# A graph transformer layer on one core: loads of node rows at most eight chunks ahead, released by ScalarE

## The chip, the cores and the metric

The kernel runs on one core of one Trainium2 chip. The metric is the device time of one execution in microseconds (us); the number given for a kernel is the median of several executions. The core has five engines that follow their own instruction queues and meet at semaphores: TensorE (PE, with its weight loads listed as PEld), VectorE (DVE), ScalarE (ACT), GpSimd (POOL) and SyncE (SP), which only issues DMAs here.

## The reference

Three layers of a graph transformer convolution over 6250 nodes with 64 features. There are 206250 directed edges, sorted by their destination; each has its own 64 attributes.

```
q = x @ Wq + bq;  k = x @ Wk + bk;  v = x @ Wv + bv;  e = edge_attr @ We
alpha = sum(q[dst] * (k[src] + e)) / sqrt(64)
p = exp(alpha - segment_max(alpha, dst)[dst])
w = p / segment_sum(p, dst)[dst]
out = segment_sum((v[src] + e) * w, dst) + x @ Ws + bs
```

Between the layers come a ReLU and a layer norm; behind the last one a log softmax, the residual and a final layer norm. What costs time is `x[src]`: for every edge and in every layer, a row of 64 numbers from a place given by the graph. The kernel works with the rows of x and the edge attributes side by side and multiplies by the weights afterwards.

## The kernel before, in words

**Tiling.** The edges are cut into 403 chunks of 512, each four tiles of 128. Four chunks are a batch (101 batches, the last of three chunks). The work runs in 102 units, a unit being a batch except at the end, where the last batch makes two; `NU` is 102, `LB` is 4, `T` is 4.

**A batch's data.** `feat` is a buffer for one batch: for each edge the row of x and the 64 attributes. There are five such buffers (`FB` = 5). `fetch` (L532) writes the attributes with one DMA of 512 KB on SyncE's queue. `gather` (L549) writes the rows of x for one chunk: for each tile of 128 edges one indirect DMA on GpSimd (L553), with the tile's 128 node numbers read from a list in SBUF, `src_a` for the first edges and `src_b` for all. These DMAs are called loads here. In layers 1 and 2 `x` is the earlier layer's output (the tile is named `x`), in layer 0 the input (`in_x`). Three tiles of a batch have no load: `pick` (L841) makes their rows from x in SBUF, with TensorE multiplying by one-hot matrices (L858, L849) and VectorE masking and adding up (L868, L871); `aim` (L818) makes the one-hot matrix `hot` (L825, L830). So a batch takes 13 loads, 15 early in layer 0, and 16 where nothing is picked, as in a layer's batch 0.

**Which load may start when.** A load must not overtake the use of the buffer that it writes. In addition the kernel holds the loads of a chunk back until a turn of TensorE has come: `release` (L569) copies the chunk's indices to a small tile `gate` (L576, VectorE, 128x4 integers; 24 such buffers), and the loads read their indices from there. So a load of GpSimd, whose queue would otherwise run ahead, waits for that copy, and the copy stands in VectorE's queue at the place where it was issued.

**A round.** The main loop (L1253) has one round `u` for each unit but the last two. The round adds up the messages of unit u-3 (`sums(u - 2)` does all units below u-2; L1150), which sets that buffer free: `room` (L1196) then issues the `fetch` of batch u+2 into it and puts its chunks on the list `pending`. It transposes the weights of unit u-2 (L1136, L1138) and makes the scores of unit u-1 (L1115 once a unit, L1117 for each chunk; L1124, L1126, L1128 are the running softmax). Then there are four turns: `turn(j)` (L1096) transposes chunk j of unit u's rows by TensorE (L1100 in layer 0, L1105 later) and copies the result to `featT` on ScalarE (L1101, L1108). Behind `turn(j)` stands `release(j+1)`, which lets chunk j of batch u+2 be loaded, eight chunks ahead of the turn. Between the turns lie parts of `pick`, `aim` and of the tasks in `step` and `close_up`. `ask` (L1063) reads a unit's queries (L1075) and `across` (L1088) moves the transposed attributes between layers, both on SyncE.

**Starts.** At the program's start, five batches are fetched and all their loads issued with no gate (L615 to L618): 79 loads. At a layer's end (L1294 to L1345) the same is done for the next layer, five batches and 68 loads, once all of the layer's output has been written. Round 0 follows, and the first batch that is gated is batch 5, in round 3.

**Order.** Each engine runs its instructions in the order in which the program issues them; nothing reorders them across engines. So the place of a call in the loop is the place of its instructions in each queue.

Of the kernel before, what the change touches and what calls it, by code (L numbers as in the profile page):

```python
# [10 lines left out]
I32 = mybir.dt.int32  # L11
# [7 lines left out]
P = 128  # L19
D = 64  # L20
L = 3
T = 4
# [9 lines left out]
LB = 4  # L32
FB = 5
# [381 lines left out]
def main_path(  # L415
# [53 lines left out]
    nc = tc.nc  # L469
# [14 lines left out]
    batches = [(c, min(LB, NC - c)) for c in range(0, NC, LB)]  # L484
    units = list(batches)
    if units[-1][1] > 1:
        c, m = units.pop()
# [15 lines left out]
    gates = ctx.enter_context(tc.tile_pool(name="gates", bufs=6 * LB))  # L503
    nodes = ctx.enter_context(tc.tile_pool(name="nodes", bufs=2))

    def ps(tag):
        return psum.tile([P, 512], F32, tag=tag, name=f"ps_{tag}", bufs={"a": 3, "x": 2}.get(tag, 1))
# [5 lines left out]
    def picked(layer, k):  # L513

        if batches[k][1] < LB or k < LEAD[layer]:
            return 0
        return 1 if layer == 0 and k <= len(groups) else PICKS
# [5 lines left out]
    HEAD = FB * LB * T  # L523
    src_a = const.tile([P, HEAD], I32, name="src_a")
    nc.sync.dma_start(src_a, src[:, :HEAD])
    src_b = const.tile([P, NC * T], I32, name="src_b")
    loaded = {}

    def fetch(layer, k):

        c0, m = batches[k]
        feat = feats.tile([P, LB * T * 2 * D], F32, name="feat")  # L532
        if layer:
            feat = feat.rearrange("p (h c t d) -> p c t h d", h=2, c=LB, d=D)
        else:
            feat = feat.rearrange("p (c t h d) -> p c t h d", h=2, c=LB, d=D)
        nc.sync.dma_start(
            feat[:, :m, :, 1].rearrange("p c t d -> p (c t) d"),
            ea[c0 : c0 + m].rearrange("c (t p) d -> p (c t) d", p=P),
        )  # L540
        loaded[layer, k] = feat

    def spots(n):

        return [(c, T - 1) for c in range(LB - n, LB)]

    def gather(layer, k, c, index, i):

        feat = loaded[layer, k]  # L549
        for t in range(T):  # L550
            if (c, t) in spots(picked(layer, k)):
                continue
            nc.gpsimd.indirect_dma_start(  # L553
                out=feat[:, c, t, 0],
                out_offset=None,
                in_=xts[layer][:, :],
                in_offset=bass.IndirectOffsetOnAxis(ap=index[:, i + t : i + t + 1], axis=0),
            )

    def gather_all(layer, k):  # L560

        c0, m = batches[k]
        index = src_a if (c0 + m) * T <= HEAD else src_b
        for c in range(m):
            gather(layer, k, c, index, (c0 + c) * T)

    pending = []

    def release(upto):  # L569

        for entry in list(pending):
            layer, k, c = entry
            c0, m = batches[k]
            while c < min(m, upto):
                gate = gates.tile([P, T], I32, name="gate")
                nc.vector.tensor_copy(gate, src_b[:, (c0 + c) * T : (c0 + c + 1) * T])  # L576
                gather(layer, k, c, gate, 0)
                c += 1
            entry[2] = c
            if c == m:  # L580
                pending.remove(entry)

    ident = const.tile([P, P], F32, name="ident")
    make_identity(nc, ident)
# [25 lines left out]
    def rows_of(g, n):  # L610
        y = nodes.tile([P, GS, D], F32, name="xr")[:, :n]
        nc.sync.dma_start(y, x[g * P : (g + n) * P, :].rearrange("(j p) d -> p j d", p=P))
        return y

    entered = {g: rows_of(g, n) for g, n in groups[:2]}  # L615
    for k in range(FB):
        fetch(0, k)
        gather_all(0, k)  # L618


    spans = dram.tile([NK * P, 2], F32, name="spans")
# [197 lines left out]
    def aim(layer, k):  # L819

        if k >= len(batches) or not picked(layer, k):
            return
        n = picked(layer, k)
        pk = ps("p")[:, : n * P]
        nc.tensor.matmul(  # L825
            pk, one[:, k : k + 1].to_broadcast([P, P]), keyT[:, (MOST - n) * P :], start=True, stop=True
        )
        for s in range(n):
            hot = picks.tile([P, NH, P], F32R, name="hot")
            nc.vector.tensor_tensor(  # L830
                hot,
                pk[:, s * P : (s + 1) * P].unsqueeze(1).to_broadcast([P, NH, P]),
                rank.unsqueeze(2).to_broadcast([P, NH, P]),
                ALU.is_equal,
            )
            hots[layer, k, s] = hot
# [85 lines left out]
    def begin(g, n):  # L922
        y = entered.get(g)
        if y is None:
            y = rows_of(g, n)
            yield
        yield from project(0, g, n, y)
# [241 lines left out]
    next(first)  # L1169
    rest = locate(0)  # L1170
    next(rest), next(rest)
    next(first, None)
    next(rest), next(rest)
    for _ in first:
        pass
    for _ in rest:
        pass
    nc.vector.tensor_copy(base, ends[:, :, 0])
    active.append(begin(*groups[1]))
    active.append(keys())  # L1180
    active.append(divide())
# [14 lines left out]
    def room(layer, k):  # L1196

        if k < len(batches):
            fetch(layer, k)
            pending.append([layer, k, 0])  # L1200
        elif layer + 1 < L and k - len(batches) < FB:
            fetch(layer + 1, k - len(batches))

# [37 lines left out]
    def close_up(n=1):  # L1241
        step(n)
        for _ in range(n):
            advance(ending)

    def some(picking):

        for _ in range(2):
            next(picking, None)

    ask(0, 0)
    chunks[0, 0].across()
    for layer in range(L):  # L1253
        line = Line(layer)
        assert not picked(layer, 0)
        aim(layer, 1)
        for u in range(NU - 2):
            close = u >= CLOSE
            this = chunks[layer, u]
            picking = pick(layer, u + 1)  # L1260
            line.sums(u - 2)
            line.weights(u - 1)
            line.scores(u)
            if waiting:
                active.append(waiting.pop(0))
            this.turn(0)
            release(1)
            close_up(2) if close else close_up()
            ask(layer, u + 1)
            chunks[layer, u + 1].across()  # L1270
            some(picking)
            aim(layer, u + 2)
            this.turn(1)
            release(2)
            line.store()
            close_up(2) if close else step()
            some(picking)
            if close:
                line.sums(u - 1)
                line.weights(u)  # L1280
            this.turn(2)
            release(3)
            line.store()
            close_up(2) if close else step()
            some(picking)
            if close:
                line.sums(u)
            line.store()
            assert next(picking, None) is None
            this.turn(3)  # L1290
            release(LB)
            close_up(2) if close else step()

        more = layer + 1 < L  # L1294
        assert not pending
        ask(layer, NU - 1)
        rest, last = chunks[layer, NU - 2], chunks[layer, NU - 1]
        line.scores(NU - 2)
        last.across()
        if more:  # L1300
            reload(layer + 1, 0)
            reload(layer + 1, 1)
            ask(layer + 1, 0)
        rest.turn(0)
        line.weights(NU - 2)
        close_up()
        for j in range(1, rest.m):
            rest.turn(j)
        if more:
            split(*held[0])  # L1310
        line.sums(NU - 2)
        line.store()
        close_up()
        line.scores(NU - 1)
        if more:
            chunks[layer + 1, 0].across()
            split(*held[1])
        line.weights(NU - 1)
        last.turn(0)
        close_up()  # L1320
        line.scores(NU)
        line.sums(NU - 1)
        line.store()
        line.weights(NU)
        line.sums(NU)
        line.store()
        while active or len(ending) > 1:
            close_up()
        if more:
            for i in range(2, len(pieces) - 1):  # L1330
                reload(layer + 1, i)
        while ending and (not more or (layer, groups[-1][0]) not in written):
            close_up()
        if more:
            assert all((layer, g) in written for g, n in groups)
            for k in range(FB):
                if (layer + 1, k) not in loaded:
                    fetch(layer + 1, k)
                gather_all(layer + 1, k)
            reload(layer + 1, len(pieces) - 1)  # L1340
            close_up()
            for i in range(2, len(pieces)):
                split(*held[i])
            while ending:
                close_up()  # L1345
# [45 lines left out]
```

## Time and profile before

| | |
|---|---|
| three executions, us | 7144.72, 7116.72, 7071.52 |
| median, us | 7116.72 |
| profiled execution, us | 7065.72 |
| its span, us | 7063.9 |
| its mean granted TensorE clock | 0.84 |
| loads by L553 without a gate | 79 in layer 0, 136 in layers 1 and 2 |
| loads by L553 with a gate | 1265 in layer 0, 2494 in layers 1 and 2 |
| gate copies by L576 | 1149 |
| one load on GpSimd, one gate copy on VectorE | 0.944 us, 0.161 us (medians) |

The profiled execution is one of its own and 0.7% below the median. In a line of the profile, the part in brackets is the time that the engine stood idle before the instruction, and what ended that. "issue" means that nothing in the profile explains the idle time, "remote" that what ended it is not an instruction that the profile shows. Of the lines that belong to the loads and to what stands beside them, these are the costliest:

```profile
L858 PE MATMUL ps_x<-parts,hot 128*128 128x512 f32 x10344 | 3109.7, 450 | 800.8 <-DVE rows_of_b L868 458.5
L553 POOL DMA_INDIRECT feat<-x,gate x2494 | 2360.8, 947 | 1944.0 <-issue 945.2
L553 POOL DMA_INDIRECT feat<-in_x,gate x1265 | 1200.2, 949 | 1038.6 <-issue 511.8
L868 DVE TENSOR_TENSOR rows_of_b<-ps_x,which 128x512 f32<-128x512 f32 x862 | 590.7, 685 | 1314.7 <-remote 863.4
L1108 ACT COPY featT<-ps_a 64x256 f32<-64x256 f32 x1612 | 589.3, 366 | 1659.2 <-remote 782.7
```

A line gives the place in the code, the engine, the operation with its tiles and shapes and how often it occurs; then its busy time in us and the mean ns of one; then the idle time of the engine just before it and what ended most of that.

### The profile page before, as it was taken

The numbers are of one execution on the slowest core, as the hardware profiler recorded it, in microseconds if no ns is written. First come the engines' busy times: TensorE is split into PE (matmuls) and PEld (weight loads), VectorE is DVE, ScalarE is ACT, GpSimd is POOL, SyncE is SP. The second block draws the span as 40 slices with busy tenths as digits, with TensorE's granted clock in tenths as the row PEclk, the third lists the DMA queues.
The fourth block names the chain that finished last, engine by engine and source line by source line (L and its number), as shares of the span: only waits on it lengthen the run. The fifth ranks groups of instructions, "written<-read, shape, count | busy, mean of one in ns | idle before, by whom it ended". The sixth has DMA issues, their size and how long they took to land.

```text
span 7063.9 us, 83912 instructions
## 1 busy us (share of the span) xinstructions
PE 5168.6 (73%) x24583; PEld 3500.1 (50%) x24583; DVE 3348.6 (47%) x6501; ACT 1369.1 (19%) x3267; POOL 3765.2 (53%) x3982
## 2 busy tenths in 40 slices
PE   3777788877787557777777777764777777877786
PEld 2355555555555345454555455443455555555553
DVE  3344544554454335444454445443455554555554
ACT  1111111111111112122121222221122222222222
POOL 4555555555555345555555555534555555555553
PEclk9688888888888779888888888877888888888887
DMA  5333333333333323333333333332333333333332
GB/s 123 92 80 79 80 79 80 78 74 79 78 80 74 75 58 83 76 79 79 77 84 77 75 74 80 77 79 50 81 73 80 79 82 75 83 77 84 83 83 59
DMA packets 1132753, 554.00 MB, mean 78 GB/s; under 512 B 946566, under 2 KB 1043964, under 8 KB 1113091
## 3 DMA queue, kind: packets, MB, share of 16 engines
q1 hardware_dynamic: 988834, 409.90, 25.3%
q0 software_dynamic: 127168, 130.47, 8.5%
q10 hardware_dynamic: 16288, 8.17, 0.5%
q8 instruction: 204, 3.34, 0.2%
q14 instruction: 259, 2.11, 0.1%
HBM read 451.48 MB, written 96.59 MB: 78 GB/s over the span
## 4 chain that ended last, share of the span: by engine, by line


## 5 line engine op out<-in xcount | busy, mean ns | idle before, releaser
L858 PE MATMUL ps_x<-parts,hot 128*128 128x512 f32 x10344 | 3109.7, 450 | 800.8 <-DVE rows_of_b L868 458.5
L553 POOL DMA_INDIRECT feat<-x,gate x2494 | 2360.8, 947 | 1944.0 <-issue 945.2
L858 PEld LDWEIGHTS ps_x<-parts,hot 128*128 128x128 f32 x10344 | 2179.0, 219 | 1421.6 <-DVE rows_of_b L868 514.3
L553 POOL DMA_INDIRECT feat<-in_x,gate x1265 | 1200.2, 949 | 1038.6 <-issue 511.8
L868 DVE TENSOR_TENSOR rows_of_b<-ps_x,which 128x512 f32<-128x512 f32 x862 | 590.7, 685 | 1314.7 <-remote 863.4
L871 DVE TENSOR_REDUCE feat<-rows_of_b 128x64 f32<-128x512 f32 x862 | 905.4, 1050 | 29.7
L1108 ACT COPY featT<-ps_a 64x256 f32<-64x256 f32 x1612 | 589.3, 366 | 1659.2 <-remote 782.7
L830 DVE TENSOR_TENSOR hot<-ps_p,rank 128x896 fp32r<-128x896 f32 x862 | 883.3, 1077 | 8.9 <-PE ps_p L825 5.6
L1150 PE MATMUL ps_g<-feat,probT 128*64 128x256 f32 x4848 | 653.0, 402 | 54.3 <-issue 33.5
L1138 DVE COPY probT<-ps_p 128x512 f32<-128x512 f32 (+2 forms) x306 | 208.5, 681 | 977.4 <-remote 606.7
L1117 PE MATMUL ps_s<-featT,q 128*32 128x512 f32 x2418 | 438.0, 641 | 269.2 <-ACT featT L1108 195.5
L1124 DVE TENSOR_REDUCE most<-ps_s 128x1 f32<-128x512 f32 (+2 forms) x306 | 210.5, 688 | 871.9 <-remote 526.8
L1150 PEld LDWEIGHTS ps_g<-feat,probT 128*64 128x64 f32 x4848 | 343.0, 142 | 288.9 <-issue 141.6
L1128 ACT ACTIVATE prob<-ps_s,part 128x512 f32<-128x512 f32 (+2 forms) x306 | 210.4, 688 | 1412.1 <-DVE part L1126 740.8
L1101 ACT COPY featT<-ps_a 128x512 f32<-128x512 f32 x403 | 228.7, 585 | 964.0 <-remote 370.3
L1105 PE MATMUL ps_a<-ident,feat 128*128 128x128 f32 x1612 | 351.6, 300 | 51.5 <-issue 24.1
L1100 PE MATMUL ps_a<-ident,feat 128*128 128x128 f32 x1612 | 287.8, 302 | 54.7 <-issue 53.1
L1105 PEld LDWEIGHTS ps_a<-ident,feat 128*128 128x128 f32 x1612 | 192.8, 150 | 267.5 <-issue 186.9
L1158 ACT COPY part<-ps_g 128x256 f32<-128x256 f32 (+2 forms) x306 | 113.8, 372 | 1047.4 <-remote 578.0
L1100 PEld LDWEIGHTS ps_a<-ident,feat 128*128 128x128 f32 x1612 | 200.8, 155 | 167.9 <-issue 134.8
L1117 PEld LDWEIGHTS ps_s<-featT,q 128*32 128x32 f32 x2418 | 62.5, 110 | 409.6 <-ACT featT L1108 229.7
L825 PE MATMUL ps_p<-keyT,one 128*128 128x384 f32 (+1 forms) x294 | 127.9, 435 | 179.0 <-DVE probT L1138 122.3
(145 smaller groups left out, 2632.6 us busy)
## 6 DMA issues: line engine op xcount, KB each, us to landing
feat<-in_ea SPq DMA_DIRECT2D x300, 512.0 KB
featT<-eaT SPq DMA_DIRECT2D x200, 512.0 KB
eaT<-featT SPq DMA_DIRECT2D x100, 512.0 KB
feat<-x,gate POOLq DMA_INDIRECT x2494
feat<-in_x,gate POOLq DMA_INDIRECT x1265
part<-part SPq DMA_DIRECT2D x1209, 16.2 KB
q<-qq SPq DMA_DIRECT2D x1209, 16.0 KB
both<-part SPq DMA_DIRECT2D x66, 260.0 KB
```

The costliest lines, as they stand in the source:

```text
L553: nc.gpsimd.indirect_dma_start(out=feat[:, c, t, 0], out_offset=None, in_=xts[layer][:, :], in_offset=bass.IndirectOffsetOnAxis(ap=index[: ...
L830: nc.vector.tensor_tensor(hot, pk[:, s * P : (s + 1) * P].unsqueeze(1).to_broadcast([P, NH, P]), rank.unsqueeze(2).to_broadcast([P, NH, P] ...
L858: nc.tensor.matmul(px[:, : b1 - b0, :].rearrange("p b d -> p (b d)"), hot[:, h, :], parts[:, i, b0:b1, :].rearrange("p b d -> p (b d)"), s ...
L868: nc.vector.tensor_tensor(rows, px, which[:, MOST - n + s, k, :].unsqueeze(2).to_broadcast([P, KB, D]), ALU.mult)
L871: nc.vector.tensor_reduce(loaded[layer, k][:, LB - n + s, T - 1, 0], rows.rearrange("p b d -> p d b"), AX.X, ALU.add)
L1100: nc.tensor.transpose(pt[:, t * P : (t + 1) * P], self.feat(j)[:, t].rearrange("p h d -> p (h d)"), ident)
L1101: nc.scalar.copy(self.featT[:, j, :], pt)
L1105: nc.tensor.transpose(pt[:, t // 2 * P : (t // 2 + 1) * P], rows[:, t * D : (t + 2) * D], ident)
L1108: nc.scalar.copy(featT[:, :, h, :], pt[h * D : (h + 1) * D, : T // 2 * P].rearrange("d (i e) -> d i e", e=P))
L1117: nc.tensor.matmul(self.p_s[j * W : (j + 1) * W, :], self.q[:, j, :], self.featT[:, j, :], start=False, stop=True)
L1124: nc.vector.tensor_reduce(top[:n], self.p_s[:n], AX.X, ALU.max)
L1150: nc.tensor.matmul(p_g[j * W : (j + w) * W, :w, :].rearrange("n c (h d) -> n c h d", h=2), self.probT[:, t, j * W : (j + w) * W], batch[:, ...
```

## The change

Three things are changed together.

- **Starts.** A layer's start issues the loads of batch 0 alone, 16 in place of 79 or 68. The other four batches are put on `pending`. In the program's start the `fetch` of batches 2 to 4 moves behind `ask(0, 0)` and `across`, and the four chunks of batch 1 are released one by one between the parts of the setup, by copies on VectorE.
- **Distance.** In the rounds, `free(u, j)` stands where `release(j+1)` stood. It releases every pending chunk whose number is below `u * 4 + j + 1 + lead`. `lead` is 8 chunks in layer 0, and the lesser of 8 and 4 + u in the others. From round 5 on this is one chunk a turn, 8 chunks ahead, as before; in rounds 1 to 4 of layers 1 and 2 it is five chunks a round, and in rounds 0 to 2, which released nothing, the chunks that a start no longer loads.
- **Engine.** The gate copies in the rounds are made by ScalarE in place of VectorE, right behind the turn's own copies in its queue.

The number of loads stays 3974. 1193 gate copies are issued on ScalarE and 4 on VectorE, where there were 1149 on VectorE. `fetch` of later batches stays where it was, in round u that of batch u+2.

```diff
+    def indices(layer, k, c):
+
+        c0, _ = batches[k]
+        if not layer and (c0 + c + 1) * T <= HEAD:
+            return src_a, (c0 + c) * T
+        return src_b, (c0 + c) * T
+
     def gather_all(layer, k):
 
-        c0, m = batches[k]
-        index = src_a if (c0 + m) * T <= HEAD else src_b
-        for c in range(m):
-            gather(layer, k, c, index, (c0 + c) * T)
+        for c in range(batches[k][1]):
+            gather(layer, k, c, *indices(layer, k, c))
 
     pending = []
 
-    def release(upto):
-
-        for entry in list(pending):
-            layer, k, c = entry
-            c0, m = batches[k]
-            while c < min(m, upto):
-                gate = gates.tile([P, T], I32, name="gate")
-                nc.vector.tensor_copy(gate, src_b[:, (c0 + c) * T : (c0 + c + 1) * T])
-                gather(layer, k, c, gate, 0)
-                c += 1
-            entry[2] = c
-            if c == m:
-                pending.remove(entry)
+    def await_turn(layer, k):
+
+        pending.extend((layer, k, c) for c in range(batches[k][1]))
+
+    def release(layer, upto, copy=nc.vector.tensor_copy):
+
+        while pending and pending[0][0] == layer and pending[0][1] * LB + pending[0][2] < upto:
+            layer, k, c = pending.pop(0)
+            index, i = indices(layer, k, c)
+            gate = gates.tile([P, T], I32, name="gate")
+            copy(gate, index[:, i : i + T])
+            gather(layer, k, c, gate, 0)
...
-    for k in range(FB):
-        fetch(0, k)
-        gather_all(0, k)
+    fetch(0, 0)
+    gather_all(0, 0)
+    fetch(0, 1)
+    await_turn(0, 1)
...
     ask(0, 0)
     chunks[0, 0].across()
+    for k in range(2, FB):
+        fetch(0, k)
+        await_turn(0, k)
     for layer in range(L):
         line = Line(layer)
         assert not picked(layer, 0)
+
+        def free(u, j):
+            lead = 2 * LB if not layer else min(2 * LB, LB + u)
+            release(layer, u * LB + j + 1 + lead, nc.scalar.copy)
+
...
             this.turn(0)
-            release(1)
+            free(u, 0)
...
             this.turn(3)
-            release(LB)
+            free(u, 3)
...
             for k in range(FB):
                 if (layer + 1, k) not in loaded:
                     fetch(layer + 1, k)
-                gather_all(layer + 1, k)
+                if k:
+                    await_turn(layer + 1, k)
+                else:
+                    gather_all(layer + 1, k)
```

More of the change, by code (lines that the diff above doesn't have):

```diff
@@ L1171, in main_path @@
     next(rest), next(rest)
+    release(0, LB + 1)
     next(first, None)
     next(rest), next(rest)
+    release(0, LB + 2)
     for _ in first:
@@ L1177, in main_path @@
         pass
+    release(0, LB + 3)
     nc.vector.tensor_copy(base, ends[:, :, 0])
+    release(0, 2 * LB)
     active.append(begin(*groups[1]))
@@ L1199, in room @@
             fetch(layer, k)
-            pending.append([layer, k, 0])
+            await_turn(layer, k)
         elif layer + 1 < L and k - len(batches) < FB:
@@ L1273, in main_path @@
             this.turn(1)
-            release(2)
+            free(u, 1)
             line.store()
@@ L1281, in main_path @@
             this.turn(2)
-            release(3)
+            free(u, 2)
             line.store()
```

## The prediction

> **What bounds the kernel now.** The busy shares of the page come first: no engine is full.
>
> ```profile
> span 7063.9 us, 83912 instructions
> PE 5168.6 (73%) x24583; PEld 3500.1 (50%) x24583; DVE 3348.6 (47%) x6501; ACT 1369.1 (19%) x3267; POOL 3765.2 (53%) x3982
> ```
>
> A round works on one batch of four chunks, and TensorE's matmul L1115 occurs once in each. Its starts give the length of a round: in layer 1 the steady stretch has 87 of them from 2651.9 to 4576.3, which is 86 rounds of 22.4 us; layers 0 and 2 give 22.4 and 21.7, the mean is 22.2. How long is a round that waits for nothing? The view of stretches answers. The first two lines below are rounds 1 and 2 of layer 1, and columns 3 on are the busy us of PE, PEld, DVE, ACT and POOL, then TensorE's granted clock and the DMA share.
>
> ```profile
> 2452.70:2540.00 87.30, 17.78 (x62) 9.76 (x61) 10.90 (x14) 5.92 (x14) 47.86 (x51) 0.57 0.12 27
> 2540.00:2553.60 13.60, 13.60 (x78) 9.88 (x77) 11.09 (x15) 4.40 (x13) 0.00 (x0) 1.00 0.16 40
> ...
> 3321.00:3324.00 3.00, 3.00 (x16) 2.50 (x15) 0.00 (x0) 0.93 (x4) 2.13 (x3) 1.00 0.42 79
> 3324.00:3331.00 7.00, 0.41 (x4) 0.17 (x2) 0.00 (x0) 0.00 (x0) 5.42 (x6) 0.88 0.26 52
> 3331.00:3334.00 3.00, 0.00 (x0) 0.00 (x0) 0.39 (x1) 0.28 (x1) 0.00 (x0) 0.50 0.61 148
> 3334.00:3338.70 4.70, 4.34 (x10) 3.48 (x11) 4.67 (x7) 1.18 (x4) 0.00 (x0) 0.50 0.05 12
> ```
>
> Round 2 has no load of rows on POOL and TensorE is busy for all of its 13.6 us. Round 1 runs beside a queue of such loads, and takes 87.3 us for 17.8 us of TensorE. The last four lines are an ordinary round that began to load at 3315.02: VectorE stops at 3321, TensorE at about 3324, and everything comes back near 3333.6. The view of single instructions shows the same place; after the start come the duration, the engine and, in brackets, the idle time and who ended it.
>
> ```profile
> 3320.02 0.94 POOL L553 DMA_INDIRECT feat<-x,gate  x1 [0.30 <-issue]
> 3320.24 0.17 DVE L576 COPY gate<-src_b 128x4 int32<-128x4 int32 x1
> ...
> 3330.00 0.94 POOL L553 DMA_INDIRECT feat<-x,gate  x1 [0.30 <-issue]
> ...
> 3333.61 0.69 DVE L868 TENSOR_TENSOR rows_of_b<-ps_x,which 128x512 f32<-128x512 f32 x1 [12.70 <-remote]
> 3333.72 1.51 ACT L1108 COPY featT<-ps_a 64x256 f32<-64x256 f32 x4 [11.33 <-remote]
> ```
>
> VectorE waited 12.70 us and ScalarE 11.33 us for nothing that the profile names ("remote"), and both resume 2.7 us after the last of an unbroken run of loads. The view of waits shows that this is the kernel's main loss:
>
> ```profile
> POOL feat L553 <- DVE gate L576: 1062.3, 259, 10.7
> DVE rows_of_b L868 <- remote: 863.4, 103, 37.5
> ACT featT L1108 <- remote: 782.7, 94, 39.9
> DVE probT L1138 <- remote: 606.7, 71, 17.0
> ```
>
> So I read the bound thus: loads cost 1.25 us each on POOL from start to start (0.94 busy plus 0.30), 13 a round, 16.25 us. A run of them lets the others work for a while, then stops them until about 2.5 us after its end. I counted the runs in the trace's list of L553 (a pause over 0.6 us ends a run): 120 runs of 4 loads, which stop hardly anything, 127 of 9, 103 of 13, 39 of 10. The 296 runs of 7 or more outside the layers' starts hold 3163 loads, 10.7 each (13.4 us). By 3759 gated loads, 13 a round, there are 289 rounds, so 1.02 long runs a round. From round = 13.5 + 1.02 x (13.4 - h + 2.5) = 22.2 the head h, in which work goes on beside loads, is 7.4 us; the row above has 6 us for VectorE and 9 for TensorE's queued work.
>
> **The change part by part**, against the profiled run's 7065.72 us; the median 7116.72 is 0.72% above it, so a result is scaled by 1.0072. A measurement of this kernel can't tell less than about 1% (71 us) from no change: the runs spread over 73 us.
>
> *The program's start.* 79 loads go out back to back from 2.9 to 101.7 us, and the first L1115 comes at 125.2. With 16 loads they end near 23 us. The chains of setup behind them were stopped for at least 38 us (the wait of L912's VectorE that ends at 85.9), at most for the 79 us of loads that go; I take -50. The four copies on VectorE there cost 0.16 us each, nothing. The moved fetches of batches 2 to 4 (SyncE, 512 KB) are needed only some 20 us a round later: nothing, or the 1 us of issue each.
>
> *Layers 1 and 2 at the start.* 68 loads become 16, and the other 52 come in the rounds. Now it is 21.5 us from the first load (2431.2) to the L1115 of round 1, that round takes 87.3 and round 2 takes 13.6; the gates begin in round 3, and 96 rounds have 13 loads: 122 + 96 x 22.2 = 2253. Afterwards round 0 has 16 + 13 loads, at least the 21.5 of now and at most 29 x 1.25 = 36; I take 35. Rounds 1 to 4 have 17 loads, four more at 0.94 to 1.25 each, so 26 to 27. 94 ordinary rounds follow. 35 + 4 x 26.4 + 94 x 22.2 = 2227: -26 a layer. Layer 0: rounds 0 to 2 get the loads that left the start, rounds 1 and 2 take 20.7 and 14.7 now and would take some 25, and round 0 some 10 more: +25 against the -50. The ends together: -25 - 2 x 26 = -77, bounds -140 and +10.
>
> *Gates on ScalarE.* 1193 copies of 128x4 int32. The nearest row of ScalarE is the small L968 (128x8 f32), 0.21 us: 250 us in all, beside other work, because ScalarE is 19% busy and the next entry of its queue (the copy of the next turn) comes some 3 us later. I take 0. If the copy is always in front of the turn's consumer it costs 4 x 0.21 a round, 240 us in all; a gain from it is excluded on ScalarE itself. Behind a gate that waits stand L1108, L1128 and L1158, and TensorE behind those; but the gate waits for the gather 24 gates earlier, six rounds back, long landed. VectorE loses 1149 x 0.16 = 186 us; it lies idle through the stalls, so I take 0, at most -150.
>
> *What that moves.* This is the part that decides. VectorE's gates stand in its queue behind the picks: in an undisturbed round they come 3.9, 9.2, 11.1 and 12.9 us after L1115, so one chunk goes alone and three go together. ScalarE's come right behind the turns' copies, at some 2.5, 5.9, 8.9 and 12.3. A chunk is 3 or 4 loads, 3.75 or 5 us of POOL, turns lie 3.05 to 4.1 us apart: each next release falls into the current run. There are no free short runs, but the run ends as soon as its stop reaches the turn that would feed it: after two chunks (7 loads) or three (10). With r runs a round, all long, round = 13.5 + 16.25 + r x (2.5 - 7.4) = 29.75 - 4.9 r. Seven loads a run: r = 13/7 = 1.86, 20.6 us. Ten: r = 1.3, 23.4 us. No row tells which; I take the middle, 22.0, 0.2 less than now: -0.2 x 289 = -58. The distance in these rounds is 8 chunks before and after (round u releases batch u+2), so only the gate's engine differs there.
>
> [...]
>
> Sum: 7066 - 77 - 58 = 6931, times 1.0072: 6980 us.
>
> **The rivals.** *A: two chunks a run.* If the stop comes early enough that runs stay at 7 loads, the round is 20.6: -1.6 x 289 - 77 = -539, 6527, or 6574 us. For it: runs of 4 now go free. Against it: a stop set in only 6 to 9 us after a run's first load, time enough for a third turn. A stronger form has no stops at all: POOL's 16.25 us bound the round, 289 x 5.95 + 77 less, about 5300 us. This would hold if the stop came from loads piled up ahead of POOL, for a turn then hands over 4 at most. The run above speaks against it: it stalled with its gates 2 us apart.
>
> [...]
>
> *B: nothing gained.* The rounds stay at 22.2, and what leaves the starts comes back: a round with 17 loads gets one more stop, 2.5 us and some 2.4 us of TensorE at half clock behind it (12 matmuls of L858 take 5.4 us there against 3.0), 5 us in each of 8 rounds. -77 + 40 = -37: 7029, or 7080 us. For it: loads back to back in a start cost (87.3 - 13.6)/68 = 1.08 us each or less, and a load that lengthens a stopped run 1.25.
>
> *C, slower: three chunks and more a run.* The short runs that are free now vanish, and each stop catches a run that three turns have already fed. The round is 23.4: +1.2 x 289 - 77 = +270, 7336, or 7389 us. For it: the head of 7.4 us is longer than two turn distances (6.4), so a third release is usually in time. Against it: the turns slow down when TensorE's clock is low, and then the run starves sooner. It is over 1% slower from (77 + 71)/289 = 0.5 us on, a round of 22.7, or 9 loads a run. After a stop the clock is 0.50 (last two rows of the stretches), and more stops make more of this.
>
> [...]
>
> **How the numbers follow.** Forecast 0.38 (round 21.5 to 22.4, so 6835 to 7100 us), A 0.20, B 0.14, C 0.28. The forecast's case splits 0.30 faster by over 1%, 0.06 within, 0.02 slower. Faster: 0.30 + 0.20 = 0.50. Same: 0.06 + 0.14 = 0.20. Slower: 0.30. The range leaves out the far half of A and less than half of C: 6520 to 7340 us.
>
> **What would show it.** First L1115 near 75 us; rounds 1 to 4 of layers 1 and 2 at about 26 us, none near 87; no wait "POOL feat <- DVE gate"; ScalarE's gate row at about 0.21 us; and, deciding between the cases, the count of runs of L553 by length: a mean of 8 to 9 loads for me, 7 for A, 10 and more for C. I am wrong if the stop has another cause than the unbroken run of loads, since all the sums per round rest on that.

## The result, and the profile after

The changed kernel takes 6712.74 us (median of 4, 6701.64 to 6724.67), the kernel before 7119.05 us (median of 4). The ratio is 0.9437, 95% interval 0.9382 to 0.9491: 406 us faster, where the prediction had 6980 us, 139 us faster. The profiled execution took 6724.67 us; all terms below compare its span with the 7063.9 us of before. The page of the changed kernel, same engines:

```profile
span 6723.0 us, 84981 instructions
...
PE 5225.9 (78%) x24583; PEld 3475.7 (52%) x24583; DVE 3220.8 (48%) x5356; ACT 1479.2 (22%) x4460; POOL 3765.4 (56%) x3982
```

GpSimd is busy for 3765 us in both, and the span is 341 us shorter: what went is time in which it stood idle. The starts of L1115 (L1120 now) tell where:

| stretch of the span | before, us | after, us | difference | forecast |
|---|---|---|---|---|
| start to the first L1115 | 125.2 | 76.3 | -48.9 | -50 |
| layer 0, first five rounds from there | 108.9 | 130.0 | +21.1 | +25 |
| layers 1 and 2, the same | 156.0, 156.2 | 128.6, 128.9 | -27.5, -27.4 | -26 each |
| steady 90 rounds of layer 0 | 2033.6 | 1922.8 | -110.7 | -18 |
| of layer 1 | 2014.9 | 1903.9 | -111.0 | -18 |
| of layer 2 | 1953.4 | 1955.4 | +2.0 | -18 |
| last six rounds of the three layers | 386.6 | 347.2 | -39.4 | within the -58 |
| between and behind the layers | 129.1 | 129.9 | +0.8 | 0 |

So the starts and the rounds next to them (the first three rows) came out as forecast, -83 us for -77. The later rounds gave 259 us in place of 58, all of it in layers 0 and 1 and in the closing rounds. Rounds 1 to 4 of layer 1, in the view of stretches of the changed kernel (columns as in the prediction):

```profile
2300.58:2328.80 28.22, 16.96 (x63) 10.07 (x62) 9.03 (x11) 5.36 (x16) 17.61 (x20) 0.82 0.24 46
2328.80:2361.00 32.20, 24.66 (x78) 12.14 (x77) 11.59 (x16) 6.08 (x22) 18.85 (x20) 0.73 0.19 37
2361.00:2382.00 21.00, 16.61 (x79) 11.20 (x78) 9.63 (x14) 4.49 (x17) 13.21 (x14) 0.84 0.40 79
2382.00:2412.00 30.00, 15.71 (x78) 11.25 (x77) 11.20 (x15) 4.19 (x15) 19.82 (x21) 0.77 0.32 64
```

No round of 87 us is left, and the four take 27.9 us on the mean (forecast about 26). An ordinary round of layer 1, single instructions of the changed kernel:

```profile
3309.66 0.19 ACT L584 COPY gate<-src_b 128x4 int32<-128x4 int32 x1
...
3315.47 0.94 POOL L553 DMA_INDIRECT feat<-x,gate  x1 [0.30 <-issue]
...
3317.43 2.20 PE L863 MATMUL ps_x<-parts,hot 128*128 128x512 f32 x3 [0.93 <-issue]
3318.89 0.38 ACT L1163 COPY part<-ps_g 128x256 f32<-128x256 f32 x1 [9.04 <-remote]
3318.95 0.69 DVE L1143 COPY probT<-ps_p 128x512 f32<-128x512 f32 x1 [8.94 <-remote]
...
3322.36 0.94 POOL L553 DMA_INDIRECT feat<-x,gate  x1 [5.94 <-ACT gate L584]
```

The stops, in which several engines wait beside a run of loads, are still there: a run of 13 loads ends at 3316.4, and ScalarE and VectorE come back 2.5 us later from waits of 9 us. The gate behind the next turn then lets the loads go on, 6 us after the run. The wait of GpSimd for its gates, which the prediction wanted gone, is still there under ScalarE's name, 1380 us where it was 1062 for VectorE's, while GpSimd's waits for "issue" went from 1521 to 1089. But TensorE was not idle for all of the stop; it worked on in small pieces to 3319.6. The view of waits:

```profile
POOL feat L553 <- ACT gate L584: 1380.5, 339, 9.4
DVE probT L1143 <- remote: 1208.1, 144, 18.6
...
ACT part L1163 <- remote: 1065.0, 124, 14.0
ACT featT L1113 <- remote: 723.9, 95, 14.7
DVE rows_of_b L873 <- remote: 652.2, 108, 17.5
```

The stops now catch VectorE and ScalarE at other instructions (L1143 and L1163 at unit u-2's weights and sums, more than the picks), and "PE ps_x L858 <- DVE rows_of_b L868", 458.5 us before, is 200.0 us (L863 <- L873).

### The profile page after: what moved, and what is told of

Its sections match the earlier page's. It is cut to its first block, busy times and chain, and to the rows that moved or that the text cites. A ratio compares the mean times of both kernels' runs of the same rounds, so it can differ in the third digit from the quotient of the medians.

```text
span 6723.0 us, 84981 instructions
## 1 busy us (share of the span) xinstructions
PE 5225.9 (78%) x24583; PEld 3475.7 (52%) x24583; DVE 3220.8 (48%) x5356; ACT 1479.2 (22%) x4460; POOL 3765.4 (56%) x3982
## 3 DMA queue, kind: packets, MB, share of 16 engines
q1 hardware_dynamic: 988834, 409.90, 27.5%
q0 software_dynamic: 127168, 130.47, 10.9%
## 4 chain that ended last, share of the span: by engine, by line
## 5 line engine op out<-in xcount | busy, mean ns | idle before, releaser
L553 POOL DMA_INDIRECT feat<-x,gate x2598 | 2457.8, 946 | 1814.2 <-ACT gate L584 910.6
L863 PE MATMUL ps_x<-parts,hot 128*128 128x512 f32 x10344 | 3041.1, 442 | 503.0 <-issue 295.4
L863 PEld LDWEIGHTS ps_x<-parts,hot 128*128 128x128 f32 x10344 | 2130.3, 214 | 1091.1 <-issue 446.3
L553 POOL DMA_INDIRECT feat<-in_x,gate x1328 | 1261.3, 950 | 920.0 <-ACT gate L584 469.8
L873 DVE TENSOR_TENSOR rows_of_b<-ps_x,which 128x512 f32<-128x512 f32 x862 | 591.5, 686 | 1437.9 <-remote 652.2
L1143 DVE COPY probT<-ps_p 128x512 f32<-128x512 f32 (+2 forms) x306 | 208.3, 681 | 1481.6 <-remote 1208.1
L1122 PE MATMUL ps_s<-featT,q 128*32 128x512 f32 x2418 | 560.5, 650 | 257.5 <-ACT featT L1113 112.3
L1163 ACT COPY part<-ps_g 128x256 f32<-128x256 f32 (+2 forms) x306 | 113.9, 372 | 1418.1 <-remote 1065.0
L1110 PE MATMUL ps_a<-ident,feat 128*128 128x128 f32 x1612 | 349.6, 301 | 13.5 <-issue 8.9
L1122 PEld LDWEIGHTS ps_s<-featT,q 128*32 128x32 f32 x2418 | 80.1, 110 | 494.1 <-issue 267.5
```

What stands on the lines that cost most here:

```text
L553: nc.gpsimd.indirect_dma_start(out=feat[:, c, t, 0], out_offset=None, in_=xts[layer][:, :], in_offset=bass.IndirectOffsetOnAxis(ap=index[: ...
L863: nc.tensor.matmul(px[:, : b1 - b0, :].rearrange("p b d -> p (b d)"), hot[:, h, :], parts[:, i, b0:b1, :].rearrange("p b d -> p (b d)"), s ...
L873: nc.vector.tensor_tensor(rows, px, which[:, MOST - n + s, k, :].unsqueeze(2).to_broadcast([P, KB, D]), ALU.mult)
L1110: nc.tensor.transpose(pt[:, t // 2 * P : (t // 2 + 1) * P], rows[:, t * D : (t + 2) * D], ident)
L1122: nc.tensor.matmul(self.p_s[j * W : (j + 1) * W, :], self.q[:, j, :], self.featT[:, j, :], start=False, stop=True)
```

## The experiments

What was open is what shortened the rounds: the gate's engine, the place of the release in the round, VectorE's relief, or the new starts. The ratios in this part are to the kernel before on the same chip in the same session; the chips were the ones numbered 3, 8, 8 and 9 in the four sessions. The chip of the result itself is not on record.

**Only the engine, in the kernel before.**

```diff
-                nc.vector.tensor_copy(gate, src_b[:, (c0 + c) * T : (c0 + c + 1) * T])
+                nc.scalar.copy(gate, src_b[:, (c0 + c) * T : (c0 + c + 1) * T])
```

> The kernel before with one edit: the gate copies of the rounds on ScalarE, the starts as they were. In the profiles the steady rounds (5 to 95 of each layer) went from 22.2 to 21.4 us and gave 220 of the 341 us. Theory 1 (the gate's engine gives the steady gain, the starts the rest): 7119 - 220 to 260, so about 6870, and rounds of 21.4. Rival (the steady gain needs the new starts, for they set where in a round the loads run): about 7119, and rounds of 22.2.

**The changed kernel with VectorE's gates.**

```diff
-            release(layer, u * LB + j + 1 + lead, nc.scalar.copy)
+            release(layer, u * LB + j + 1 + lead)
```

> The changed kernel with one edit: the gate copies of the rounds on VectorE again. Theory 1: the starts alone are left, 120 us less than before, so about 7000, and rounds of 22.2. Rival (starts set the phase): about 6713, rounds of 21.4.

**ScalarE's gates, and a spare copy on VectorE.**

```diff
             copy(gate, index[:, i : i + T])
+            if copy == nc.scalar.copy:
+                spare = gates.tile([P, T], I32, name="spare")
+                nc.vector.tensor_copy(spare, index[:, i : i + T])
```

> The changed kernel, and VectorE makes a spare copy of the same 128x4 integers, read by nobody, where its gate copy stood; the loads still wait for ScalarE's. Theory 1a (it is the place and time of the release that counts): within 1% of 6713. Theory 1b (it is VectorE's relief, 4 x 0.16 us and four instructions a round): back up by 200 us or more, above 6900.

Measured: 0.9995 (0.9985 to 1.0004), 0.9990 (0.9980 to 0.9999) and 0.9990 (0.9981 to 1.0000). No expectation was met, because the kernel before itself took 5175.79 us here (median of 25), where it had taken 7119.05. Nothing follows for the theories: the loss that they divide was not there. The first of the three, waits:

```profile
ACT featT L1108 <- PE ps_a L1105: 1472.1, 556, 6.9
POOL feat L553 <- issue: 975.7, 3201, 0.3
DVE rows_of_b L868 <- PE ps_x L849: 889.3, 513, 10.0
```

No "remote" wait leads the list, VectorE and ScalarE wait for TensorE by name, and GpSimd's unnamed waits are 0.3 us each, the step from one load to the next: within a layer it loads nearly without a pause, and nothing stops. Rounds are 16.3 us, which is 13 x 1.25.

**Pauses in the runs**, a GpSimd copy of a number just loaded, behind every second chunk:

```diff
             gather(layer, k, c, gate, 0)
+            if c % 2:
+                seen = gates.tile([P, 1], F32, name="seen")
+                nc.gpsimd.tensor_copy(seen[:1], loaded[layer, k][:1, c, T - 2, 0, :1])
```

> The changed kernel, and GpSimd copies one number of the rows just loaded behind every second chunk in the rounds, which makes it wait for that load to land: runs of at most 7 or 8 loads, with a pause of some 1 to 2.5 us. Theory: long unbroken runs of loads are what stops the other engines (runs of 7 keep TensorE busy for 10.4 of 10.5 us in the changed kernel's trace): rounds of 16.25 + 2 x 1.8 = 19.9, so 6713 - 289 x 1.5 = about 6280. Rival 1 (a pause of about 2 us with waiting in it does not end the stop): rounds of 21.4 + 2 x 1.8, 7700. Rival 2 (the copies only lengthen GpSimd's time and stops stay as frequent): 6900 to 7300.

Measured: 1.2873 (1.2850 to 1.2897), 6659.92 us. Where nothing stops, it has only its price:

```profile
POOL feat L553 <- issue: 1083.2, 3630, 2.1
POOL seen L588 <- DMA feat<-x,gate: 943.1, 390, 5.2
PE ps_a L1113 <- DMA feat<-x,gate: 930.1, 680, 5.1
...
POOL seen L588 <- DMA feat<-in_x,gate: 364.5, 195, 6.2
```

585 waits for a landing, 2.2 us each, and then TensorE waits for rows. What a pause does to a stop was not seen.

**The changed kernel itself, and three variants, on a second chip.** `f1` is the changed kernel. `f2` and `f3` are the first two experiments again. `f4` releases all four chunks of a round behind turn 0:

```diff
-            release(layer, u * LB + j + 1 + lead, nc.scalar.copy)
+            release(layer, u * LB + LB + lead, nc.scalar.copy)
```

> The changed kernel unaltered, to see on which chips its gain is there. In the first four experiments the kernel before itself took 5176 us, with rounds of 16.3 us, no 'remote' waits and GpSimd loading without a pause. Theory S (the gain belongs to the stops, and whether stops occur belongs to the chip or its setting, not to the kernel): where the kernel before takes about 7100, 6713; where it takes about 5176, within 0.5% of it. Rival (the stops go with the kernel as it is built and laid out): any mixture.

> The kernel before with gates on ScalarE, once more. Where the kernel before takes about 7100. Theory 1 (gate's engine gives the steady gain): about 6870, steady rounds 21.4. Rival (the starts set it): 7119, rounds 22.2. Where it takes 5176: 0.9995 of it, as measured.

> The changed kernel with gates on VectorE again, once more. Where the kernel before takes about 7100. Theory 1: about 7000, steady rounds 22.2. Rival: 6713, rounds 21.4. Where it takes 5176: 0.999 of it, as measured.

> The changed kernel, but all four chunks of a round are released behind turn 0, one run of 13 loads a round. Where stops occur: by the prediction's formula (29.75 - 4.9 x 1 run) a round of 24.9, so about 7730; by what a run of 13 did in the changed kernel's trace (16 us of run with 12.9 us of TensorE's work in it, then a pause of 5.7) a round of 21.7, so about 6800. Where none occur: GpSimd loads without a pause either way, 0.999 of the kernel before.

Measured: 0.9988 (0.9977 to 1.0000), 0.9994 (0.9983 to 1.0006), 0.9984 (0.9972 to 0.9995), 0.9990 (0.9979 to 1.0001), the kernel before at 5177.57 us. The changed kernel's page here, and layer 1's steady 90 rounds as a stretch:

```profile
PE 4554.7 (88%) x24583; PEld 3176.9 (62%) x24583; DVE 3267.8 (63%) x5356; ACT 1492.4 (29%) x4460; POOL 3775.2 (73%) x3982
```

```profile
1882.60:3347.60 1465.00, 1323.56 (x7211) 927.71 (x7211) 971.02 (x1510) 440.98 (x1420) 1108.36 (x1171) 0.98 0.52 108
```

1465 us against the 1903.9 of the result's profile, with the same instructions on GpSimd (1171 loads here, 1174 there) and the same duration of each. So the half of theory S that could be seen holds: without stops the change is worth 0.1%, and neither the gate's engine nor the order of release counts, because GpSimd has its next load at hand at nearly all times: it waits 59.5 us for its gates here, 1380.5 in the result's profile. Its other half, the change with stops on another occasion, was not seen. As the result's chip is not known, it is open whether the stops go with the chip or with something else in that session; the kernel alone does not bring them.

**Once more, and the bound tested by the number of loads.** `g1`, `g2` and `g3` repeat the kernels with VectorE's gates, with spare copies and with one release, in case stops came back; the chip was number 8 again. `g4` picks two tiles in place of three (`PICKS = 2`), so a round has 14 loads.

> The changed kernel with the gates of the rounds on VectorE again, on a further chip. Two chips so far had no stops. If this one has them (the kernel before at about 7100): the gate's engine is worth 220 us or more of the 406 (so about 6950) by theory 1, nothing (6713) by its rival. If it has none: 0.999 of the kernel before, and the stops were found on none of three chips.

> The changed kernel with spare copies on VectorE, read by nobody. With stops: 6713 if the place of the release counts, above 6900 if VectorE's relief counts. Without: 0.999 of the kernel before.

> All four chunks of a round released behind turn 0. With stops: 7730 by the prediction's formula (24.9 us a round), 6800 by what runs of 13 did in the changed kernel's trace (21.7). Without: 0.999 of the kernel before.

> The changed kernel with two tiles of a batch picked by TensorE in place of three, so 14 loads a round and one block of 12 matmuls (3.0 us) less for TensorE. Without stops, if GpSimd's loads bound the round (13 x 1.25 = 16.25 of 16.3): 17.55 us a round, 5170 + 290 x 1.25 = about 5530. Rival (TensorE, 88% busy, bounds it): 3 us less a round, or no change. With stops: 14 loads lengthen the runs by 1.25 and TensorE's work falls by 3.0, within 200 us of 6713.

Measured: 0.9991 (0.9979 to 1.0002), 0.9995 (0.9983 to 1.0007), 0.9992 (0.9981 to 1.0004): no stops again. `g4`: 1.0634 (1.0572 to 1.0696), 5493.31 us, rounds of 17.6 in layers 1 and 2 (1580 us for 90), where the changed kernel had 16.3: one load more, 1.3 us more, though TensorE had 3 us less to do. So GpSimd's loads bound the changed kernel where nothing stops.

**Fewer loads, on a third chip**, with two of the variants again. `h3` picks four tiles in even batches and three in odd ones:

```diff
-        return 1 if layer == 0 and k <= len(groups) else PICKS
+        return 1 if layer == 0 and k <= len(groups) else PICKS - k % 2
...
+            some(picking)
             assert next(picking, None) is None
```

(with `PICKS = 4`, and 8 gate buffers in place of 24 for room).

> The changed kernel with the gates of the rounds on VectorE. With stops (the kernel before at about 7100): 6950 if the gate's engine gave the steady gain, 6713 if the starts did. Without: 0.999 of the kernel before.

> The changed kernel with spare copies on VectorE. With stops: 6713 if the place of the release counts, above 6900 if VectorE's relief does. Without: 0.999 of the kernel before.

> The changed kernel with four tiles picked in every even batch and three in every odd one (12.5 loads a round, 15.6 us; 8 gate buffers in place of 24 to make room). Without stops: if the loads are the bound and TensorE's 13.5 us plus half a pick (1.7) stay below it, 0.6 us a round less, 5165 - 290 x 0.6 = about 4990. Rival: TensorE's extra pick ends last, and rounds stay at 16.3 or grow, 5165 to 5400. With stops: below 6713 by up to 180 if GpSimd's time counts there.

Measured: 0.9988 (0.9977 to 1.0000), 0.9995 (0.9983 to 1.0006), no stops; `h3`: 0.9823 (0.9794 to 0.9851), 5071.26 us. Its page:

```profile
PE 4803.9 (95%) x26417; PEld 3454.6 (68%) x26417; DVE 3652.6 (72%) x5779; ACT 1490.7 (29%) x4460; POOL 3648.8 (72%) x3841
```

Rounds are 15.7 us in layers 1 and 2, which is 12.5 x 1.25 and near the expected 15.6, and 16.5 in layer 0, which gained nothing (16.3 in the changed kernel on chip 8): there a turn has four transposes in place of two, and TensorE is busy for 1467 of the 1487 us of the steady rounds, as the rival had it. In layer 1 it is busy for 1404 of 1412 us, so a further pick would find no room there either. The gain over the kernel before is 1.8%, about half of what was expected. Where there are stops, it was not run.

## Why the prediction was off, point by point

- **The start, -50:** right; -48.9. Without stops the same first L1115 comes at 61.3 us with 79 loads in front (chip 3, gates on ScalarE) and at 67.8 with 16 (chip 8). So what the start gained was its stop, as the step said.
- **Layers 0 to 2 behind their starts, +25 and -26 each:** right; +21.1, -27.5, -27.4.
- **Gates on ScalarE cost nothing:** a copy takes 0.19 us (0.21 forecast) and nothing in the profile shows a wait for it on ScalarE. On chips without stops, 0.9995 for the engine alone bounds its price to 0.1%. Where stops occur, it wasn't isolated.
- **"I take the middle, 22.0", -58:** this is the term that failed. The steady rounds went from 22.2 to 21.4 and, with the closing rounds, gave -259. The step put all of it on the number of long runs a round, and took runs of 4 loads to "stop hardly anything". By the count of L553's runs in the trace of after, 332 runs of 7 or more hold 3630 loads: 10.9 each, as long as before (10.7), not the 8.5 taken; 1.10 a round over 302 rounds. With the head h = 7.4 us that is 13.5 + 1.10 x (13.7 - 7.4 + 2.5) = 23.2, rival C. So the runs came out as in rival C, which was to be slower, and the kernel was faster.
- **What the formula left out** can be counted on GpSimd, where the length of a round is its loads times 1.25 us plus the pauses between runs (less the 0.30 that each pause replaces). In the 270 steady rounds, the pauses behind runs of 7 or more add up to 1293 us before (280 pauses) and 1317 after (303). Those behind shorter runs add up to 436 us before (143 pauses) and 170 after (75): 266 us, more than all of the 220 that the steady rounds gave. So the gain lies in the pauses behind short runs, which the formula put at nothing: short runs joined longer ones, 423 pauses became 378, and the prediction had priced this as rival C's loss. In 105 of the 143 no late update of TensorE (below) is recorded: there GpSimd waited for its next gate with no sign of a stop. To give 21.4, the formula would need h = 9.0; but beside a run of 13 loads and 2.5 us on, TensorE starts 63.3 matmuls after (116 runs) and 61.4 before (103 runs), so little more work goes on there.
- **Layer 2** gives nothing, 21.7 before and after. GpSimd's pauses add up to 5.8 us a round there, 5.9 before; in layers 0 and 1 they fell from 6.6 to 5.4 and 5.3. The pauses behind short runs fell in layer 2 too, from 119 to 49 us in its 90 rounds, but those behind runs of 7 or more rose from 416 to 476: it has the most runs of 13 loads after the change (55, against 31 in layer 1). Why it came to longer runs than the other layers, no run showed. Which part of the change took the short runs' pauses away, the gate's engine, the place of the release, VectorE's relief or the new starts, remains open: no session after the first pair showed a stop.
- **Rival A's stronger form**, no stops and rounds of GpSimd's 16.25 us, about 5300 us, is what chips 3, 8 and 9 measured, but for the kernel before as well. On those chips GpSimd had its next load at hand nearly all through a layer (two runs of 1315 loads and one of 1175 in the changed kernel on chip 8), and no other engine stood still (the first experiment has no "remote" wait among its 22 largest), so loads piled up ahead of GpSimd alone are no cause of the stops.
- **"I am wrong if the stop has another cause than the unbroken run of loads":** it has, at least, a second condition. Far longer runs (of up to 1315 loads on chip 8) stopped nothing on three chips.
- **"Nothing that the profile names":** the trace does name it. Each of the 512 "remote" waits of over 2 us of VectorE, ScalarE and GpSimd in the trace of before, 4105 us in all, ended with an update of the semaphore on which TensorE counts its finished work. In the round that the prediction shows, TensorE has this gap:

```profile
3324.02 0.39 PE L1105 MATMUL ps_a<-ident,feat 128*128 128x128 f32 x2
...
3334.36 2.08 PE L858 MATMUL ps_x<-parts,hot 128*128 128x512 f32 x4 [9.96 <-DVE rows_of_b L868]
```

Seven of its instructions that make such an update ended from 3320.92 to 3324.41, and seven updates stand in the trace from 3333.59 to 3333.90, just where VectorE and ScalarE resume. So they did not wait for nothing: they waited for TensorE's word, which came up to 13 us behind its work. The prediction's mechanism fits this in part. Of the places where four or more updates come over 2 us late (233 before, 211 after) none lies within a run of loads, and nine in ten lie 1.4 to 2.8 us behind the end of one. What holds the updates up, no run shows.

## What to carry to other kernels

A wait that the profile can't name ("remote"), and that falls on several engines at once, is worth a second session, on another chip, before a kernel is fitted to it: this change was worth 5.6% where the stops were, and 0.1% where they were not. Look also at which semaphore the wait is for, and when the instruction that updates it ended. Sums made from stretches that were measured as a whole (the starts) held to a few us; a formula with a constant fitted to one schedule, and with nothing for the short runs, did not survive the change of that schedule. Where one engine issues work without a pause, count its instructions: one load more a batch lengthened the rounds of layers 1 and 2 by 1.3 us, and half a load less shortened them by 0.6, but layer 0 by nothing, because there TensorE was full (busy for 1467 of the 1487 us of the steady rounds).

## What the runs showed of the hardware that was not expected

The two profiles with stops have all instructions, but a third of the updates of semaphores: 42,578 recorded in the kernel before and 40,217 in the changed one, against 129,527 for the changed kernel on a chip without stops. On average that is 6.0 a us in both (42,578/7064; 40,217/6723), and 25 without (129,527/5165). It is no steady rate: in steps of 1 us it goes from 0 to 82 in the kernel before, and to 85 without stops.

In the same two profiles TensorE's updates come late: 2031 of 5206 recorded ones in the kernel before, and 1918 of 5116 in the changed one, stand over 2 us behind the end of the last TensorE instruction that makes one, by up to 41 us. In each of the 15 profiles without stops two do, of over 5800, and the median is 0.014 us. VectorE's and ScalarE's own updates come about 0.01 us behind their instructions (medians) in all 17. Stops, missing records and late updates came together in two profiled executions of two; which causes which, or what third thing causes them, was not tried.
